# Second scores spread and attention transposed through DRAM scratch instead of TensorE, in a four-layer graph kernel

## The chip, the cores and the metric

The kernel runs on one core of a Trainium2 chip. The metric is the device time in microseconds (us), as the median of repeated executions. Everything is float32: the input holds 128 graphs of 128 nodes with 512 features each (32 MB), and the output has the same size.

## The reference, cut to what matters

Four graph layers run one after the other, each with a residual and a layer normalisation. The change touches layer 2, an attention layer, and what runs beside it.

```python
# layer 0: x = LN(x + adj @ x @ W0 + bias)
# layer 1: x = LN(x + rel @ v), rel = norm(adj.T * (q @ k.T)), q, k, v = x @ Wq.T, x @ Wk.T, x @ Wv.T
# layer 2 (a: 1024 numbers, mask = adj):
h = einsum('bnc,cf->bnf', x, W)
s1 = einsum('bnf,f->bn', h, a1)
s2 = einsum('bnf,f->bn', h, a2)
e = leaky_relu(s1[:, :, None] + s2[:, None, :], negative_slope=0.2)
e = e * mask[None, :, :]
att = softmax(e, axis=2)
h_prime = einsum('bij,bjf->bif', att, h)
x = LN(x + elu(h_prime + beta * h))
# layer 3: x = LN(x + max over features of relu(...))
```

In layer 2 the scores `s2[j]` have to stand along the free axis on all 128 partitions, because `e[i, j] = s1[i] + s2[j]` has node `i` on the partitions. The product `att @ h` needs the attention transposed, with `j` on the partitions. Both are moves of data across partitions.

## The kernel before: the parts concerned

The graphs are worked on in 32 groups of 4 (`G = 4`, `NG = 32`). Each group passes through all layers, and the groups are staggered: in one period of 28 table slots the kernel runs layer 0 of one group, layer 1 of the group before it, and layers 2 and 3 of earlier ones. `TABLE` gives for each step the slot, relative to the group's own start, at which its instructions are emitted; step `f` of group `g` is emitted at `28 * g + slot`. All pieces are then sorted by slot, and each engine keeps its instructions in that order. So slot 61.6 of group g, slot 33.6 of group g+1 and slot 5.6 of group g+2 are neighbours in every engine's queue.

```python
    TABLE = dict(
        load=[-20], y=row(0.5, 1), bias=row(1.3, 1), y_sums=row(5.2, 0.5), y_w=row(7, 1, 7),
        ...
        move=row(20.5, 0.1), x_sums=row(25.3, 0.5), m=row(28, 1, 7), scores=row(36.5, 1),
        masked=[39.95], squares=[40.4], turn_rel=[40.3],
        move_rel=row(41.2, 0.1), inverse=[42.5], v=row(42, 1, 7), attend=row(50.6, 1),
        residual=row(51.0, 1), dots=[51.7, 53.8, 54.9, 55.6], norm1=[54.6], scale=[57.2],
        apply1=row(65.4, 0.33),
        spread=[61.6], leaky=[62.0], weighted=[63.4], greatest=[64.3], exps=[64.4],
        divide=[65.8], turn_att=[68.6], with_beta=[69.0], gather=row(71.5, 1),
        z_sums=row(75.3, 0.5), z_w=row(77, 1, 7), exp=[87.5, 88.5, 90.4, 92.0],
        elu=[87.8, 89.4, 92.8, 93.8], norm2=[95.0], apply2=row(95.7, 0.33),
        ...
    )
```

The four large products (`y`, `m`, `v`, `z`) are done by a Strassen-like scheme of seven block products each. A block product is a step of 8 matmuls; its result goes to one of three regions, and the regions live in few PSUM buffers. In the steps' order 1, 2, 6, 5, 7, 3, 4, region 1 (step 2) and region 2 (steps 5 and 3) share a single buffer, `r12`, across all four products.

```python
    ORDER = (1, 2, 6, 5, 7, 3, 4)
    REGION = {1: 0, 6: 0, 7: 0, 4: 0, 2: 1, 5: 2, 3: 2}
    ...
        def step(i):
            ...
            if first:                                   # i in (1, 2, 5)
                r[where] = psum.tile([P, 2, H], FP,
                    tag="r0" if where == 0 else "r12", ...,
                    bufs=2 if where == 0 else 1)
            mul(r[where], s["f"][i], bw[w][i], first)   # 8 matmuls

        def out(i):
            p, dst = r[REGION[i]], c(*BLOCK[i])
            if fresh and i in (1, 6, 5, 4):
                act.copy(dst, p)
            else:
                dve.tensor_tensor(dst, p, dst, ALU.add)

        for n, i in enumerate(ORDER):
            emit(at[n], step, i)
            emit(at[n] + 0.72, out, i)
```

GpSimd forms the sums of blocks that the scheme needs (`y_sums`, `x_sums`, `z_sums`, four 128x512 operations per product). Layer 2 before the change:

```python
        def spread():                                   # TensorE: s2 onto all partitions
            s["p"] = bank(f"p_s2_{g}")
            for b in range(G):
                pe.transpose(s["p"][:, b * P : (b + 1) * P],
                    s12[g][:, 1, b : b + 1].to_broadcast([P, P]), ident)

        def leaky():
            e = work.tile([P, G, P], FP, tag="e", ...)
            dve.tensor_tensor(e, s["p"]..., s12[g][:, 0, :, None].to_broadcast([P, G, P]), ALU.add)
            dve.scalar_tensor_tensor(e, e, ALPHA, e, op0=ALU.mult, op1=ALU.max)

        def weighted():
            pool.tensor_tensor(s["e"], s["e"], adj_b, ALU.mult)

        def greatest():
            dve.tensor_reduce(s["nm"], s["e"], AX.X, ALU.max, negate=True)

        def exps(i):                                    # ScalarE: exp and its sum, one graph each
            ...
        def divide(i):
            dve.reciprocal(rs, s["sums"]...)
            engine = pool if n == G else dve            # GpSimd, but for the last group
            engine.tensor_tensor(e, e, rs[:, :, None].to_broadcast([P, n, P]), ALU.mult)

        def turn_att(i):                                # TensorE: attention transposed
            for b in ...:
                pe.transpose(s["p"][:, b * P : (b + 1) * P], s["e"][:, b, :], ident)

        def with_beta(i):
            dve.tensor_tensor(s["eT"]..., s["p"]..., beta_b..., ALU.add)

        def gather(b):                                  # TensorE: att @ x
            ...
        def elu(b):                                     # layer 2's end, VectorE
            dve.scalar_tensor_tensor(x, s["c", b], 0.0, x2[g][:, b, :], op0=ALU.max, op1=ALU.add)
            dve.scalar_tensor_tensor(x, s["m", b], 1.0, x, op0=ALU.min, op1=ALU.add)
            stats(s, f"2_{g}", b, x)                    # batch-norm statistics of the row
```

Of the kernel before, what the change touches and what calls it, by code (L numbers as in the profile page):

```python
# [8 lines left out]
FP = mybir.dt.float32  # L9
AF = mybir.ActivationFunctionType  # L10
ALU = mybir.AluOpType
# [18 lines left out]
def kernel(  # L30
# [33 lines left out]
    pe, dve, act, pool = (InOrder(tc, e) for e in (nc.tensor, nc.vector, nc.scalar, nc.gpsimd))  # L64
    sync = InOrder(tc, nc.sync)
    B, N, D = x.shape
    P = 128
    assert N == P and D % P == 0
    K = D // P
    Q = P // 32  # L70
    H = D // 2
    G = 4
    NG = B // G
# [4 lines left out]
    work = ctx.enter_context(tc.tile_pool(name="work", bufs=1))  # L78
    small = ctx.enter_context(tc.tile_pool(name="small", bufs=4))
    psum = ctx.enter_context(tc.tile_pool(name="psum", bufs=1, space=bass.MemoryType.PSUM))  # L80

    def bank(name):
        return psum.tile([P, D], FP, tag="ps", name=name, bufs=3)
# [40 lines left out]
    ident = const.tile([P, P], FP)  # L124
# [15 lines left out]
    beta_i = const.tile([P, P], FP)  # L140
# [79 lines left out]
    def emit(at, f, *args):  # L220
        pieces.append((at, lambda: f(*args)))

    def each(at, f):
        for b in range(len(at)):
            emit(at[b], f, b)

    def row(at, step, n=G):
        return [at + i * step for i in range(n)]


    TABLE = dict(
        load=[-20], y=row(0.5, 1), bias=row(1.3, 1), y_sums=row(5.2, 0.5), y_w=row(7, 1, 7),
        stats0=row(14.4, 0.4), norm0=[16.2], apply0=row(16.8, 0.33),
        turn=row(21.4, 1), turn_blocks=row(18.4, 0.6),
        move=row(20.5, 0.1), x_sums=row(25.3, 0.5), m=row(28, 1, 7), scores=row(36.5, 1),
# [1 line left out]
        move_rel=row(41.2, 0.1), inverse=[42.5], v=row(42, 1, 7), attend=row(50.6, 1),  # L237
        residual=row(51.0, 1), dots=[51.7, 53.8, 54.9, 55.6], norm1=[54.6], scale=[57.2],
        apply1=row(65.4, 0.33),
        spread=[61.6], leaky=[62.0], weighted=[63.4], greatest=[64.3], exps=[64.4],  # L240
        divide=[65.8], turn_att=[68.6], with_beta=[69.0], gather=row(71.5, 1),
        z_sums=row(75.3, 0.5), z_w=row(77, 1, 7), exp=[87.5, 88.5, 90.4, 92.0],
        elu=[87.8, 89.4, 92.8, 93.8], norm2=[95.0], apply2=row(95.7, 0.33),
        widen=[98.7, 100.0, 103.6, 104.6], top=[99.1, 100.4, 104.0, 105.0],
# [13 lines left out]
            greatest=[10.5], exps=[11.2], divide=[13.6], turn_att=[18.3], with_beta=[18.9],  # L258
            gather=row(36.7, 0.9), z_sums=row(39.95, 1.3),
# [6 lines left out]
            m=[0.0, 1.73, 3.46, 5.2, 7.4, 9.1, 10.8], scores=row(12.7, 0.9), masked=[16.4],  # L266
# [3 lines left out]
            greatest=[52.4], exps=row(53.2, 0.6), divide=row(53.9, 0.6),  # L270
            turn_att=row(54.4, 0.6), with_beta=row(54.9, 0.6), gather=[55.2, 56.1, 60.5, 65.0],
# [98 lines left out]
    def rows_of(t):  # L370
        return lambda nh, ch: t()[:, 2 * nh : 2 * nh + 2, H * ch : H * ch + H]


    def stats(s, g, b, t):
        if b == 0:
            s["mv"] = small.tile([P, G, 2], FP, tag="mv", name=f"mv_{g}", bufs=6)
        st = small.tile([P, 6], FP, tag="st", name=f"st_{g}_{b}")
        dve.bn_stats(st, t)
        dve.bn_aggr(s["mv"][:, b, :], st)
# [235 lines left out]
    s12 = {}  # L615
# [3 lines left out]

    def layer2(g, t):  # L620
        s = {}

        def spread():
            s["p"] = bank(f"p_s2_{g}")
            for b in range(G):
                pe.transpose(
                    s["p"][:, b * P : (b + 1) * P],
                    s12[g][:, 1, b : b + 1].to_broadcast([P, P]),
                    ident,
                )  # L630

        def leaky():
            e = work.tile([P, G, P], FP, tag="e", name=f"e_{g}")
            dve.tensor_tensor(
                e,
                s["p"].rearrange("p (b n) -> p b n", b=G),
                s12[g][:, 0, :, None].to_broadcast([P, G, P]),
                ALU.add,
            )
            dve.scalar_tensor_tensor(e, e, ALPHA, e, op0=ALU.mult, op1=ALU.max)  # L640
            s["e"] = e
# [5 lines that stand above are left out]
            s["nm"] = small.tile([P, G], FP, tag="nm", name=f"nm_{g}")  # L647
            dve.tensor_reduce(s["nm"], s["e"], AX.X, ALU.max, negate=True)

        def exps(i):  # L650
            if i == 0:
                s["sums"] = small.tile([P, G], FP, tag="sums", name=f"sums_{g}")
            for b in range(i * n, i * n + n):
                act.activation(
                    s["e"][:, b, :],
                    s["e"][:, b, :],
                    AF.Exp,
                    bias=s["nm"][:, b : b + 1],
                    accum_out=s["sums"][:, b : b + 1],
                )  # L660

        def divide(i):
            rs = small.tile([P, n], FP, tag=f"rs{n}", name=f"rs_{g}_{i}")
            dve.reciprocal(rs, s["sums"][:, i * n : i * n + n])
            e = s["e"][:, i * n : i * n + n, :]
            engine = pool if n == G else dve
            engine.tensor_tensor(e, e, rs[:, :, None].to_broadcast([P, n, P]), ALU.mult)

        def turn_att(i):
            if i == 0:  # L670
                s["p"] = bank(f"p_eT_{g}")
            for b in range(i * n, i * n + n):
                pe.transpose(s["p"][:, b * P : (b + 1) * P], s["e"][:, b, :], ident)

        def with_beta(i):
            if i == 0:
                s["eT"] = work.tile([P, G, P], FP, tag="eT", name=f"eT_{g}")
            dve.tensor_tensor(
                s["eT"][:, i * n : i * n + n, :],
                s["p"].rearrange("p (b n) -> p b n", b=G)[:, i * n : i * n + n, :],  # L680
                beta_b[:, i * n : i * n + n, :],
                ALU.add,
            )

        def gather(b):
            if b == 0:
                s["zT"] = work.tile([P, K, G * P], FP, tag="aT_yz", name=f"zT_{g}")
            p = bank(f"p_z_{g}_{b}")
            for k in range(K):
                pe.matmul(  # L690
                    p[:, k * P : (k + 1) * P],
                    x2[g][:, b, k * P : (k + 1) * P],
                    s["eT"][:, b, :],
                    start=True,
                    stop=True,
                )
            act.copy(
                s["zT"][:, :, b * P : (b + 1) * P], p.rearrange("p (k n) -> p k n", k=K)
            )

        def begin():
            s["c"] = work.tile([P, G, D], FP, tag="c", name=f"c_{g}")
            for b in range(G):
                s["c", b] = s["c"][:, b, :]

        def direct(b):

            s["c", b] = psum.tile([P, D], FP, tag="r0", name=f"c_{g}_{b}", bufs=2)
            for k in range(K):
                pe.matmul(  # L710
                    s["c", b],
                    s["zT"][:, k, b * P : (b + 1) * P],
                    w2_sb[:, k, :],
                    start=(k == 0),
                    stop=(k == K - 1),
                )

        def exp(b):
            s["m", b] = work.tile([P, D], FP, tag="m", name=f"m_{g}_{b}", bufs=3)
            act.activation(s["m", b], s["c", b], AF.Exp)  # L720

        def elu(b):
            if b == 0:
                x3[g] = data.tile([P, G, D], FP, tag="x3", name=f"x3_{g}")
            x = x3[g][:, b, :]
            dve.scalar_tensor_tensor(
                x, s["c", b], 0.0, x2[g][:, b, :], op0=ALU.max, op1=ALU.add
            )
            dve.scalar_tensor_tensor(x, s["m", b], 1.0, x, op0=ALU.min, op1=ALU.add)
            stats(s, f"2_{g}", b, x)  # L730

        n = G // len(t["exps"])
        emit(t["spread"][0], spread)
        emit(t["leaky"][0], leaky)
        emit(t["weighted"][0], weighted)
        emit(t["greatest"][0], greatest)
        each(t["exps"], exps)
        each(t["divide"], divide)
        each(t["turn_att"], turn_att)
        each(t["with_beta"], with_beta)  # L740
        each(t["gather"], gather)
        if g < NG - 1:
            left_factors(t["z_sums"], s, "zT", "s_yz", f"z_{g}", 0)
            product(t["z_w"], f"z_{g}", by_rows, s, "2", rows_of(lambda: s["c"]), True, begin)
        else:
            each(t["z_w"], direct)
        each(t["exp"], exp)
        each(t["elu"], elu)
        norm(t["norm2"], t["apply2"], s, f"2_{g}", lambda: x3[g])
# [107 lines left out]
```

## Time and profile before

| | before |
|---|---|
| median of 3 | 2218.47 us (2218.12 to 2219.33) |
| profiled span | 2214.6 us |
| mean granted TensorE clock | 0.996 |
| TensorE busy | 2170.9 us, 98% |
| VectorE busy | 1547.9 us, 70% |
| ScalarE busy | 1102.5 us, 50% |
| GpSimd busy | 907.7 us, 41% |
| transposes of `s2` (`p_s`) | 128 instructions |
| transposes of the attention (`p_eT`) | 128 instructions |

Engines are named PE (TensorE matmul), PEld (its weight load), DVE (VectorE), ACT (ScalarE), POOL (GpSimd) and SP (the engine that issues DMAs). In a row of the timeline the columns are the start in us, the time from the first instruction's start to the last one's end in us, the engine, a helper's line number (always the same here, so rows are told apart by tile names), the operation, output and inputs by the program's tile names, the shape, and the number of instructions merged in the row. A bracket at the end gives the idle time of the engine before the row and whom it waited for. Matmuls overlap their neighbours, so the time that a row takes on TensorE is the distance from its start to the next row's start, not its listed duration.

The tile names in the timeline: `r_m`, `r_y`, `r_v`, `r_z` are the PSUM regions of the four large products; `tT` is the result of `m`, `x` that of `y`; `s_y` and `yT` are what GpSimd's sums for `y` write; `p_s` and `p_eT` are the two groups of transposes; `e` is the attention.

### The profile page before, as it was taken

What the parts mean: (1) busy time and instruction counts of PE and PEld (TensorE: products, weight loads), DVE (VectorE), ACT (ScalarE), POOL (GpSimd) and SP (SyncE); (2) the same over time, 40 slices, a digit from 0 to 9 for tenths busy, and PEclk for the clock granted to TensorE, in tenths of its full rate; (3) what the DMA queues carried; (4) which work ended last, traced back from release to release, by engine and by line L of the source; (5) the groups of instructions that cost most, each with busy time, mean ns of one, the idle gap of its engine ahead of it and who ended that gap; (6) DMA issues with size and microseconds to landing.
All of it is one profiled execution on the core that took longest, in us unless ns stands there. A gap on an engine that the chain in (4) does not pass through costs nothing.

```text
span 2214.6 us, 31863 instructions
## 1 busy us (share of the span) xinstructions
PE 2170.9 (98%) x11073; PEld 1839.6 (83%) x11073; DVE 1547.9 (70%) x3290; ACT 1102.5 (50%) x2446; POOL 907.7 (41%) x743
## 2 busy tenths in 40 slices
PE   7999999999999999999999999999999999999996
PEld 5788888888888888888888888888888888888873
DVE  4657766767766767776767776767767677667676
ACT  2224445554445554445554445554455554455547
POOL 3334444334444344443344443344443344443321
PEclk9999999999999999999999999999999999999998
DMA  4011222211222211222112222112222112221101
GB/s 167 25 20 29 61 60 62 62 20 49 60 60 63 58 21 52 59 61 62 44 31 56 58 62 63 41 30 59 58 62 63 29 39 62 59 63 44 21 28 57
DMA packets 333295, 115.15 MB, mean 52 GB/s; under 512 B 297424, under 2 KB 297552, under 8 KB 333136
## 3 DMA queue, kind: packets, MB, share of 16 engines
q1 hardware_dynamic: 331936, 110.77, 19.7%
q10 hardware_dynamic: 1200, 2.36, 0.3%
q8 instruction: 88, 1.44, 0.3%
q14 instruction: 71, 0.58, 0.1%
HBM read 39.65 MB, written 33.55 MB: 33 GB/s over the span
## 4 chain that ended last, share of the span: by engine, by line
PE 93%; DVE 3%; ACT 2%; POOL 1%; issue 1%; DMA 0%; ACTq 0%; DVEq 0%; POOLq 0%
PE r_y L26 17%; PE r_v L26 17%; PE r_m L26 17%; PE r_z L26 17%; PE p_z L26 5%; PE p_rel L26 5%; PE p_y L26 5%; PE p_o L26 5%; PE p_a L26 5%; DVE x L26 1%; ACT x L26 1%; DVE st L26 1%; PE p_eT L26 1%; PE p_m L26 1%; PE p_s L26 1%
## 5 line engine op out<-in xcount | busy, mean ns | idle before, releaser
L26 ACT ACTIVATE x<-x,nmean,rstd 128x512 f32<-128x512 f32 x384 | 288.6, 808 | 120.8 <-DVE nmean L26 120.8
L26 DVE BATCH_NORM_STATS2 st<-x 128x6 f32<-128x512 f32 x384 | 263.8, 687 | 8.8
L26 POOL TENSOR_TENSOR x<-x,bias_sb 128x512 f32<-128x512 f32 x128 | 170.1, 1331 | 137.9 <-PE p_y L26 137.5
L26 DVE SCALAR_TENSOR_TENSOR x<-m,x 128x512 f32<-128x512 f32 x128 | 114.4, 894 | 108.5 <-ACT m L26 98.5
L26 POOL TENSOR_TENSOR s_x<-xT 128x512 f32<-128x512 f32 x64 | 82.2, 1285 | 261.1 <-DMA xT<-xB 250.2
L26 ACT COPY c<-r_z 128x512 f32<-128x512 f32 x124 | 71.2, 574 | 223.3 <-PE r_z L26 198.0
L26 ACT COPY yT<-p_y 128x512 f32<-128x512 f32 x128 | 75.1, 586 | 213.6 <-PE p_y L26 213.6
L26 POOL TENSOR_TENSOR rstd<-ve,mhalf 128x4 f32<-128x4 f32 (+1 forms) x99 | 98.5, 995 | 194.1 <-DVE ve L26 188.9
L26 DVE TENSOR_TENSOR x<-r_y,x 128x512 f32<-128x512 f32 x224 | 151.7, 678 | 31.2 <-PE r_y L26 31.0
L26 DVE SCALAR_TENSOR_TENSOR scr<-x,wa 128x512 f32<-128x512 f32 x256 | 161.5, 675 | 0.0
L26 DVE STREAM_TRANSPOSE xB<-x 128x512 f32<-128x512 f32 x120 | 81.2, 696 | 108.7 <-ACT x L26 97.7
L26 PEld LDWEIGHTS p_y<-adjT,x 128*128 128x128 f32 x1024 | 136.9, 196 | 11.2 <-ACT adjT L26 4.8
L26 POOL TENSOR_TENSOR s_z<-zT 128x512 f32<-128x512 f32 x31 | 39.4, 1270 | 255.9 <-ACT zT L26 255.9
L26 PE MATMUL p_y<-adjT,x 128*128 128x128 f32 x1024 | 137.6, 280 | 4.5 <-ACT adjT L26 4.5
L26 PEld LDWEIGHTS p_z<-eT,x 128*128 128x128 f32 x1024 | 134.0, 192 | 7.9 <-issue 1.0
L26 PEld LDWEIGHTS p_rel<-xT,tT 128*128 128x128 f32 x1024 | 134.1, 191 | 7.4 <-DVE tT L26 0.8
L26 DVE TENSOR_REDUCE mx<-p_a 128x1 f32<-128x512 f32 x128 | 88.3, 691 | 69.6 <-PE p_a L26 69.6
L26 PE MATMUL p_a<-x,adjT 128*128 128x512 f32 x256 | 130.8, 596 | 5.8 <-DVE mx L26 4.4
L26 ACT COPY tT<-r_m 128x512 f32<-128x512 f32 x128 | 75.6, 590 | 121.6 <-PE r_m L26 121.6
L26 PE MATMUL p_rel<-xT,tT 128*128 128x128 f32 x1024 | 134.9, 275 | 0.6 <-DVE tT L26 0.6
L26 PE MATMUL p_z<-eT,x 128*128 128x128 f32 x1024 | 134.7, 275 | 0.1
L26 PE MATMUL p_o<-v,relT 128*128 128x512 f32 x256 | 130.4, 593 | 0.3 <-ACT v L26 0.3
(129 smaller groups left out, 5268.6 us busy)
## 6 DMA issues: line engine op xcount, KB each, us to landing
out_dram<-x SPq DMA_DIRECT2D x128, 256.0 KB, 2.5
x<-in_x_dram SPq DMA_DIRECT2D x31, 1024.0 KB, 5.3
xT<-xB SPq DMA_DIRECT2D x480, 64.0 KB, 2.3
relT<-relB SPq DMA_DIRECT2D x512, 16.0 KB, 1.8
w_sb<-in_L_gnn_weight_dram ACTq DMA_DIRECT2D x1, 1024.0 KB, 5.6
x<-in_x_dram SPq DMA_DIRECT2D x4, 256.0 KB, 7.8
wq_sb<-in_L_gnn_Wq_dram SPq DMA_DIRECT2D x1, 1024.0 KB, 12.3
wk_sb<-in_L_gnn_Wk_dram SPq DMA_DIRECT2D x1, 1024.0 KB, 15.1
```

What stands on the lines that cost most here:

```text
L26: return lambda *args, **kw: self.tc.keep_in_program_order(op(*args, **kw))
```

## The change

For the groups 0 to 29 (the last two keep the old way, `late`), the eight transposes of each group leave TensorE. The scores `s2` are written to a 2 KB line in DRAM and read back with the same line on all partitions. The attention is divided and given its `beta * identity` in one VectorE pass (four instructions, which takes the division off GpSimd), transposed in 32x32 blocks by VectorE, written to DRAM and read back with the blocks exchanged, so that the whole 128x128 matrices come out transposed. To make room for the transfers, `spread` moves from slot 61.6 to 57.3, the softmax's steps go about one slot forward, and GpSimd's third and fourth sums for `y` go behind the mask product `weighted`. What it is for: TensorE is the busiest engine, and it is relieved of 240 of its 256 transposes in layer 2.

```diff
+    dram = ctx.enter_context(tc.tile_pool(name="dram", bufs=2, space=bass.MemoryType.DRAM))
...
-        load=[-20], y=row(0.5, 1), bias=row(1.3, 1), y_sums=row(5.2, 0.5), y_w=row(7, 1, 7),
+        load=[-20], y=row(0.5, 1), bias=row(1.3, 1), y_sums=[5.2, 5.7, 6.9, 7.4], y_w=row(7, 1, 7),
...
-        spread=[61.6], leaky=[62.0], weighted=[63.4], greatest=[64.3], exps=[64.4],
-        divide=[65.8], turn_att=[68.6], with_beta=[69.0], gather=row(71.5, 1),
+        spread=[57.3], leaky=[61.2], weighted=[62.1], greatest=[63.1], exps=[63.2],
+        divide=[64.8], turn_att=[68.6], with_beta=[69.0], turn_blocks_2=[65.4], move_2=[65.5], gather=row(71.5, 1),
...
     def layer2(g, t):
+        late = g >= NG - 2
         def spread():
-            s["p"] = bank(f"p_s2_{g}")
-            for b in range(G): pe.transpose(...)
+            if late:
+                ...                                     # as before
+            else:
+                line = dram.tile([P, G], FP, tag="s2", name=f"s2d_{g}")
+                sync.dma_start(line, s12[g][:, 1, :])
+                wide = work.tile([P, P, G], FP, tag="s2", name=f"s2_{g}")
+                sync.dma_start(
+                    wide.rearrange("p n b -> p (n b)"),
+                    line.rearrange("n b -> (n b)")[None, :].to_broadcast([P, P * G]),
+                )
+                s["s2"] = wide.rearrange("p n b -> p b n")
...
         def divide(i):
             dve.reciprocal(rs, s["sums"][:, i * n : i * n + n])
+            if not late:
+                for b in range(G):
+                    e = s["e"][:, b, :]
+                    dve.scalar_tensor_tensor(
+                        e, e, rs[:, b : b + 1], beta_i, op0=ALU.mult, op1=ALU.add
+                    )
+                return
...
+        def turn_blocks():
+            s["eB"] = work.tile([P, Q, G, P // Q], FP, tag="eB", name=f"eB_{g}")
+            dve.transpose(
+                s["eB"].rearrange("p q b u -> p b q u"),
+                s["e"].rearrange("p b (q u) -> p b q u", q=Q),
+            )
+
+        def move():
+            m = P // Q
+            blocks = dram.tile([P, Q, G * m], FP, tag="eB", name=f"eBd_{g}")
+            sync.dma_start(blocks, s["eB"].rearrange("p q b u -> p q (b u)"))
+            eT = work.tile([P, Q, G, m], FP, tag="eT", name=f"eT_{g}")
+            for q in range(Q):
+                sync.dma_start(
+                    eT[q * m : (q + 1) * m].rearrange("p a b u -> p a (b u)"),
+                    blocks.rearrange("(a j) q n -> q j a n", a=Q)[q],
+                )
+            s["eT"] = eT.rearrange("p a b u -> p b a u")
...
-        each(t["turn_att"], turn_att)
-        each(t["with_beta"], with_beta)
+        if late:
+            each(t["turn_att"], turn_att)
+            each(t["with_beta"], with_beta)
+        else:
+            emit(t["turn_blocks_2"][0], turn_blocks)
+            emit(t["move_2"][0], move)
```

## The prediction

> **What bounds it.** I read the page's busy shares and chain first, then the timeline of TensorE over one period, then VectorE and GpSimd over the stretch in which the change moves things.
>
> ```profile
> PE 2170.9 (98%) x11073; PEld 1839.6 (83%) x11073; DVE 1547.9 (70%) x3290; ACT 1102.5 (50%) x2446; POOL 907.7 (41%) x743
> ...
> PE 93%; DVE 3%; ACT 2%; POOL 1%; issue 1%; DMA 0%; ACTq 0%; DVEq 0%; POOLq 0%
> ```
>
> TensorE is busy 98% of the span and makes 93% of the chain. A busy share can hide stalls, so I add up a period. The first `p_s` transpose of a group starts at 987.8 us and that of the next at 1054.4, about 66.8 us later. In the timeline a block product takes 1.73 us from start to next start, a pair of `p_a` or `p_o` 0.86, eight matmuls of `p_y`, `p_rel` or `p_z` 0.89. A period holds 28 block products (48.4), four pairs each of `p_a` and `p_o` (6.9), four eights of each of the three others (10.7) and the transposes (0.9): 66.9 us. The whole period is TensorE's own work; there is no stall in it.
>
> TensorE's timeline in one period:
>
> ```profile
> 1052.68 1.89 PE L26 MATMUL r_m<-s_x,m_qk 128*128 128x256 f32 x8
> 1054.40 0.60 PE L26 MATMUL p_s<-ident,d 128*128 128x128 f32 x4
> 1054.84 1.89 PE L26 MATMUL r_m<-xT,t_m 128*128 128x256 f32 x8
> 1056.57 3.62 PE L26 MATMUL r_y<-w_sb,yT 128*128 128x256 f32 x16
> ...
> 1070.50 0.60 PE L26 MATMUL p_eT<-ident,e 128*128 128x128 f32 x4
> 1070.94 1.89 PE L26 MATMUL r_y<-t,yT 128*128 128x256 f32 x8
> ```
>
> Four `p_s` take 1054.84 - 1054.40 = 0.44 us, four `p_eT` likewise. What matters below: the rows of 1052.68 are step 3 of `m` (region 2), those of 1054.84 step 4, and the sixteen at 1056.57 are steps 1 and 2 of `y`. Step 2 of `y` starts at 1056.57 + 1.73 = 1058.30, and its region shares the one `r12` buffer with region 2 of `m`. So it may start only when VectorE has read step 3 of `m` out. VectorE's timeline:
>
> ```profile
> 1052.95 0.69 DVE L26 TENSOR_TENSOR tT<-r_m,tT 128x512 f32<-128x512 f32 x1 [1.15 <-PE r_m L26]
> 1053.56 0.70 DVE L26 SCALAR_TENSOR_TENSOR x<-c,x 128x512 f32<-128x512 f32 x1
> 1054.36 1.57 DVE L26 SCALAR_TENSOR_TENSOR x<-m,x 128x512 f32<-128x512 f32 x1
> 1055.96 0.69 DVE L26 BATCH_NORM_STATS2 st<-x 128x6 f32<-128x512 f32 x1
> 1056.69 0.18 DVE L26 BATCH_NORM_AGGREGATE mv<-st 128x2 f32<-128x6 f32 x1
> 1056.79 0.66 DVE L26 TENSOR_TENSOR tT<-r_m,tT 128x512 f32<-128x512 f32 x1
> 1057.37 0.68 DVE L26 TENSOR_TENSOR e<-p_s,d 128x512 f32<-128x512 f32 x1
> 1058.08 0.76 DVE L26 SCALAR_TENSOR_TENSOR e<-e 128x512 f32<-128x512 f32 x1
> 1058.76 0.68 DVE L26 TENSOR_TENSOR x<-r_y,x 128x512 f32<-128x512 f32 x1
> ```
>
> The read-out of step 3 is the `tT` of 1056.79, done at 1057.45: 0.85 us before step 2 of `y` wants the buffer. The `tT` of 1052.95 (step 7) had to wait for TensorE, so VectorE cannot be early here. From there to 1075 it has hardly a gap. GpSimd beside it:
>
> ```profile
> 1052.43 1.28 POOL L26 TENSOR_TENSOR s_y<-yT 128x512 f32<-128x512 f32 x1
> 1053.79 1.59 POOL L26 TENSOR_TENSOR s_y<-s_y,yT 128x512 f32<-128x512 f32 x1
> 1055.34 1.72 POOL L26 TENSOR_TENSOR yT<-yT 128x512 f32<-128x512 f32 x1
> 1057.02 1.27 POOL L26 TENSOR_TENSOR s_y<-yT,s_y 128x512 f32<-128x512 f32 x1
> 1058.92 1.27 POOL L26 TENSOR_TENSOR e<-e,adj_sb 128x512 f32<-128x512 f32 x1 [0.63 <-DVE e L26]
> ```
>
> **What the skill says.** The Trainium skill, "SBUF — State Buffer", section "Who interferes with whom": a VectorE instruction with two SBUF inputs and a GpSimd instruction that reads SBUF exclude each other, and the loser waits for the whole instruction. The trace agrees: `x<-m` takes 1.57 instead of 0.69 us and goes on when the second sum ends, about 1055.34; the sums take 1.59 and 1.72 instead of 1.27. "TensorE: Matmul & The Clock Gate", section "Part 4: PE-mode transpose", gives about 275 ns for a transpose in one kernel. The row here has 273 ns, but 0.44 / 4 = 0.11 us is what one takes of the pipeline, and I count that. "DMA: Bandwidth & Descriptors", section "Two DMAs through the same engine are not ordered", says that a dependent DMA has to wait for the first one's completion semaphore; so each detour costs two landings in a row. No run here shows such a pair yet. Single landings were 1.8 us (16 KB, `relT`), 2.3 (64 KB, `xT`) and 2.5 (256 KB, `out`).
>
> **The change part by part.** Removed on TensorE: 30 groups x 8 transposes x 0.11 = 26.4 us. With nothing else, 2192.1 us, 1.2% less; this is the most that it can bring.
>
> The `s2` detour: `d` is ready at 1045.03 (the last small VectorE step on `d` starts at 1044.86). Write of 2 KB, say 2 us, then read of 256 KB, 2.5 us, and some 0.6 us of issue each: there by 1051. VectorE wants it at 1053.56. Hidden, with 2 to 3 us in hand.
>
> `leaky` goes from slot 62.0 to 61.2, and the read-out of step 3 of `m` stands at 61 + 0.72 = 61.72, the `elu` pass of the second graph at 61.4. So in VectorE's order the two `leaky` instructions come in front of `x<-c`, `x<-m`, the statistics and that read-out. From start to next start they took 0.71 + 0.68 = 1.39 us. The read-out ends at 1057.45 + 1.39 = 1058.84, while TensorE, with `p_s` gone, comes to step 2 of `y` at 1058.30 - 0.44 = 1057.86. That is a stall of 1.0 us where there was none.
>
> Then the shared port. `leaky`'s first instruction now has both inputs in SBUF and runs at 1053.56 to 1054.25; the second sum gets in behind it and ends about 1055.35. The second `leaky` instruction has two SBUF inputs and waits for that, until about 1055.95 (it takes the collision that `x<-m` had). Now `weighted` is free to start on GpSimd, just as `x<-c` runs: it starts about 1056.6 and ends about 1057.75, and `x<-m` waits for it, some 0.9 us again. So two collisions in place of one: the read-out ends near 1059.8, and the stall is about 1.9 us.
>
> Behind it VectorE gets more work in the same stretch: four divisions for 128x128 (I take 0.2 us each, an estimate from the four 128x128 transposes `relB` in 0.90 us) and a 128x512 block transpose (0.70 as `xB`), with the wait for the reciprocal some 1.7 us, in front of the read-outs of steps 6, 5 and 7 of `y`. Counted from the start A of step 2 of `y`, with TensorE's rows: step 3 of `y` at A + 10.5, its buffer read out at A + 10.2; step 4 at A + 12.2, the read-out it waits for (step 7, behind a 1.0 us `rstd` on GpSimd) at A + 12.2. Zero to 0.2 us more; I take 0.1. `with_beta` (0.67) goes, but only after that.
>
> The attention's detour: blocks transposed at about A + 6.7, write landed at A + 9.2, four reads issued 0.6 to 0.7 us apart as the `relT` ones are (16 in 11.3 us), landed at A + 14. `gather` comes at A + 18.3. Hidden. The `relT` transfers start up to 2 us later; their data is needed 23 us after.
>
> Sum per group: -0.88 + 1.9 + 0.1 = +1.1 us; over 30 groups +33 us: 2251 us. Since TensorE has no slack anywhere in the period, a stall of this kind is not made good later.
>
> **Rivals.** (1) The stall does not come, and the transposes' 26 us are simply gained: 2192 us. For it: TensorE's share, and the care with which the slots were moved. Against it: the order of instructions and the single `r12` buffer are fixed by the program, and 1.39 + 0.44 is more than the 0.85 us in hand. (2) The stall comes without a second collision, because `weighted` slips in elsewhere: 1.0 + 0.1 - 0.88 = +0.2, 2225 us. Only the order of arrival at the port speaks for it. (3) A DMA becomes the bound: if the broadcast read, in which 128 partitions read the same 2 KB, takes 3 us longer than thought, `leaky` and all behind it slip and each us costs 30 us: 2280 us or more. Against it: transfers are idle in this stretch (DMA share 0.00 from 1052.68 to 1058.29), and the margins are 2 to 4 us. (4) VectorE becomes the bound over the whole stretch of `y`, with several small stalls: 2265 us.
>
> **Range and chances.** 2251 us. The range of 8 in 10 goes from 2206, between the rivals 1 and 2, to 2272, a stall of 2.7 us. Faster by 2% would be 2174, below what the removal can give: 0.02. Slower by 2% is 2263, a stall of 2.4 us: 0.25. The rest, 0.73, is within 2%.
>
> **What would show it.** Right: `p_s` and `p_eT` keep 8 instructions each; TensorE has about 30 waits `r_y` on VectorE's `tT`, some 50 to 60 us in total; a period of about 68 us; `e<-e` or `x<-m` at 1.5 us beside GpSimd's `s_y` and `e`. Wrong: no such wait and a period of 66.0 us, or waits of `p_z` on `eT` or of VectorE's `e` on the DMA of `s2`.

## The result, and the profile after

| | before | after |
|---|---|---|
| median | 2218.9 us (2218.12 to 2219.41) | 2276.58 us (2275.22 to 2277.93) |
| ratio | 1 | 1.026 (95% interval 1.0242 to 1.0278) |
| profiled span | 2214.6 us | 2273.5 us |
| TensorE busy | 2170.9 us, 98% | 2170.3 us, 95% |
| granted TensorE clock, mean | 0.996 | 0.991 |
| steady period of a group | 66.81 us | 68.64 us; 69.94 us for five groups |

The kernel became 57.7 us slower (2276.58 - 2218.9). That lies 4.6 us above the top of the predicted range.

The page after, its busy shares and its chain by engine:

```profile
PE 2170.3 (95%) x10833; PEld 1821.9 (80%) x10833; DVE 1595.8 (70%) x3410; ACT 1099.5 (48%) x2446; POOL 895.3 (39%) x713
...
PE 88%; DVE 7%; ACT 2%; issue 1%; POOL 1%; DMA 1%; ACTq 0%; DVEq 0%; POOLq 0%
```

TensorE has 240 matmuls less (11073 - 10833), yet its listed busy time is the same: its other rows have become longer by about as much. VectorE has come from 3% to 7% of the chain. The page's group of the first two steps of `y` says where:

```profile
L26 PE MATMUL r_y<-w_sb,yT 128*128 128x256 f32 x512 | 126.5, 391 | 62.3 <-DVE tT L26 62.3
```

TensorE idles 62.3 us in front of this group, released by VectorE's `tT`, in 30 waits. In a typical period TensorE's timeline reads:

```profile
1357.53 1.89 PE L26 MATMUL r_y<-w_sb,yT 128*128 128x256 f32 x8
1361.49 1.99 PE L26 MATMUL r_y<-w_sb,yT 128*128 128x256 f32 x8 [2.08 <-DVE tT L26]
1363.32 1.05 PE L26 MATMUL p_rel<-xT,tT 128*128 128x128 f32 x8
...
1371.18 1.05 PE L26 MATMUL p_rel<-xT,tT 128*128 128x128 f32 x8
1372.17 1.97 PE L26 MATMUL r_y<-w_sb,s_y 128*128 128x256 f32 x8
1374.05 1.99 PE L26 MATMUL r_y<-t,yT 128*128 128x256 f32 x8
1375.88 1.89 PE L26 MATMUL r_v<-wvT,xT 128*128 128x256 f32 x8
```

Before, steps 1 and 2 of `y` were one unbroken row of sixteen. Now step 2 starts at 1361.49 instead of 1357.53 + 1.73 = 1359.26: 2.23 us late (the bracket's 2.08 counts from the modelled end of the row before). Smaller losses follow. Step 2 itself, the first block product after the wait, takes 1.83 instead of 1.73 us: 0.10. The last `p_rel` takes 0.99 instead of 0.89, and steps 3 and 4 take 1.88 and 1.83: 0.35 together. VectorE's timeline beside it:

```profile
1354.34 0.69 DVE L26 TENSOR_TENSOR tT<-r_m,tT 128x512 f32<-128x512 f32 x1 [1.15 <-PE r_m L26]
1354.95 1.06 DVE L26 TENSOR_TENSOR e<-s,d 128x512 f32<-128x512 f32 x1
1356.05 1.60 DVE L26 SCALAR_TENSOR_TENSOR e<-e 128x512 f32<-128x512 f32 x1
...
1358.35 1.57 DVE L26 SCALAR_TENSOR_TENSOR x<-m,x 128x512 f32<-128x512 f32 x1
...
1360.78 0.66 DVE L26 TENSOR_TENSOR tT<-r_m,tT 128x512 f32<-128x512 f32 x1
```

The two `leaky` rows (`e<-s,d` and `e<-e`) now stand in front of the read-out of step 3 of `m` (1360.78), the addition with which VectorE takes the finished product out of PSUM and so frees the `r12` buffer. Two rows are long, 1.60 and 1.57 us. On GpSimd the second sum and the mask product run at those moments:

```profile
1355.18 1.91 POOL L26 TENSOR_TENSOR s_y<-s_y,yT 128x512 f32<-128x512 f32 x1
1357.72 1.65 POOL L26 TENSOR_TENSOR e<-e,adj_sb 128x512 f32<-128x512 f32 x1 [0.63 <-DVE e L26]
```

`e<-e` is held up by the first of these until about 1357.0, `x<-m` by the second until about 1359.3; undisturbed both take 0.69 us.

### The profile page after: what moved, and what is told of

Read it like the earlier page. It is cut to its first block, busy times and chain, and to the rows that moved or that the text cites. A ratio compares the mean times of both kernels' runs of the same rounds, so it can differ in the third digit from the quotient of the medians.

```text
span 2273.5 us, 31832 instructions
## 1 busy us (share of the span) xinstructions
PE 2170.3 (95%) x10833; PEld 1821.9 (80%) x10833; DVE 1595.8 (70%) x3410; ACT 1099.5 (48%) x2446; POOL 895.3 (39%) x713
## 4 chain that ended last, share of the span: by engine, by line
PE 88%; DVE 7%; ACT 2%; issue 1%; POOL 1%; DMA 1%; ACTq 0%; DVEq 0%; POOLq 0%
PE r_v L26 16%; PE r_z L26 16%; PE r_m L26 16%; PE r_y L26 15%; PE p_rel L26 5%; PE p_z L26 5%; PE p_y L26 5%; PE p_o L26 5%; PE p_a L26 4%; DVE x L26 3%; DVE st L26 2%; DVE tT L26 1%; ACT x L26 1%; ACT tT L26 1%; PE p_m L26 1%
## 5 line engine op out<-in xcount | busy, mean ns | idle before, releaser
L26 DVE TENSOR_TENSOR x<-r_y,x 128x512 f32<-128x512 f32 x224 | 150.9, 675 | 57.5 <-PE r_y L26 57.3
L26 PE MATMUL r_y<-w_sb,yT 128*128 128x256 f32 x512 | 126.5, 391 | 62.3 <-DVE tT L26 62.3
L26 PEld LDWEIGHTS r_y<-w_sb,yT 128*128 128x128 f32 x512 | 95.6, 192 | 86.2 <-DVE tT L26 74.3
```

Of the source, the lines that this page charges most:

```text
L26: return lambda *args, **kw: self.tc.keep_in_program_order(op(*args, **kw))
```

## The experiments

The theory from the prediction: TensorE waits for the single `r12` buffer, since `leaky` stands in front of its read-out, and collisions with GpSimd at the port to SBUF that both share stretch that. The rivals: the landing of the DRAM transfers sets the pace, or VectorE's added work does, wherever it stands. All runs were compared with the kernel before on the same chip.

| run | what differs | median, us | ratio to before (95%) |
|---|---|---|---|
| changed kernel | | 2276.58 | 1.0242 to 1.0278 |
| `order_back` | `leaky`, `greatest`, `exps` behind the read-outs | 2277.81 | 1.0251 to 1.0285 |
| `slots_alone` | new slots, no DRAM | 2253.6 | 1.0143 to 1.0173 |
| `unit_stride` | scores laid out graph by graph | 2470.64 | 1.112 to 1.1154 |
| `divide_late` | divisions and block transpose later | 2260.69 | 1.0175 to 1.0206 |
| `sum_behind` | one GpSimd sum later | 2243.34 | 1.0099 to 1.013 |
| `old_slots` | old slots, divisions later | 2232.32 | 1.0047 to 1.008 |
| `best_try` | the same, two graphs' `exp` and `elu` earlier | 2199.32 | 0.9899 to 0.9928 |
| `best2` | the same, block transpose later still | 2196.71 | 0.9886 to 0.9916 |
| `before_early` | kernel before, `exp` and `elu` earlier | 2217.3 | 0.9988 to 1.0005 |
| `scores_only` | only the scores through DRAM | 2208.17 | 0.9936 to 0.9965 |
| `attention_only` | only the attention through DRAM | 2203.3 | 0.9916 to 0.9949 |

### order_back: the three steps put back behind the read-outs

```diff
-        leaky=[61.2], weighted=[62.1], greatest=[63.1], exps=[63.2],
+        leaky=[61.8], weighted=[62.1], greatest=[63.8], exps=[63.9],
```

> Changed kernel with only the places of three steps put back behind the read-outs: leaky 61.2 to 61.8 (behind the read-out of step 3 of m), greatest 63.1 to 63.8 and exps 63.2 to 63.9 (behind that of step 1 of y). Theory 1 (TensorE waits for the r12 buffer because leaky stands in front of the read-out): the 30 waits of r_y step 2 on tT, 2.2 us each, are gone; what is left are waits of about 1.5 us per group at steps 7, 3 and 4 of y, because VectorE now has the four divisions and the block transpose in front of their read-outs; time near 2238 us. Theory 2 (the DRAM detour's landing times or VectorE's added work as a whole set the period): leaky later makes all behind it later, 2276 us or more.

Measured 2277.81 us: no gain. It looks like theory 2, but TensorE's timeline shows more:

```profile
1358.66 3.62 PE L26 MATMUL r_y<-w_sb,yT 128*128 128x256 f32 x16
...
1367.36 1.05 PE L26 MATMUL p_rel<-xT,tT 128*128 128x128 f32 x8
1370.49 1.97 PE L26 MATMUL r_y<-t,yT 128*128 128x256 f32 x8 [2.08 <-DVE x L26]
```

The wait at step 2 of `y` is gone, as theory 1 says: the sixteen are one row again. In its place step 7 waits for the read-out of step 6, 2.24 us (1370.49 - 1367.36 - 0.89). On VectorE this read-out stands behind a `x<-c` of 1.78 us and behind the divisions and the block transpose:

```profile
1364.27 1.78 DVE L26 SCALAR_TENSOR_TENSOR x<-c,x 128x512 f32<-128x512 f32 x1
...
1367.89 1.14 DVE L26 SCALAR_TENSOR_TENSOR e<-e,rs,beta_i 128x128 f32<-128x128 f32 x4
...
1369.06 0.71 DVE L26 STREAM_TRANSPOSE eB<-e 128x512 f32<-128x512 f32 x1
1369.70 0.65 DVE L26 TENSOR_TENSOR x<-r_y,x 128x512 f32<-128x512 f32 x1
```

The `x<-c` is long because GpSimd's last sum runs beside it:

```profile
1364.21 1.28 POOL L26 TENSOR_TENSOR s_y<-yT,s_y 128x512 f32<-128x512 f32 x1
```

This collision is new: with `leaky` later, the mask product and the two sums behind it come later too. It makes 1.10 of the 2.24 us (1.78 - 0.68); without it the read-out would still be 1.1 us late, behind the divisions and the block transpose. So the order in front of step 3's read-out is one cause, and VectorE's added work is a second one. In the changed kernel the second costs 0.35 us; that the first stall hides the rest there, since VectorE catches up while TensorE stands still, is read from the two timelines and was not tested. The expectation had put 1.5 us at these steps, without the collision.

### slots_alone: the new slots without any DRAM

```diff
-        late = g >= NG - 2
+        late = True
-        spread=[57.3], leaky=[61.2], ...
+        spread=[60.9], leaky=[61.2], ...
```

> Only the new slots, no DRAM: all groups keep both sets of transposes on TensorE (spread at 60.9, so that the scores are there for leaky at 61.2). Theory 1 (order alone makes the stall): the wait at step 2 of y comes all the same, about 1.6 us per group (leaky's first instruction reads PSUM and takes 0.7 instead of 1.07 us), nothing is removed from TensorE, and the divisions stay on GpSimd so that there are no waits at steps 3 and 4: 2218 + 30 x 1.6 = 2266 us. Theory 2 (DRAM detour is the cause): no wait, 2218 us.

Measured 2253.6 us, 34 us more than before with not one DMA added. The wait is at the same place:

```profile
1344.38 1.89 PE L26 MATMUL r_y<-w_sb,yT 128*128 128x256 f32 x8
1347.26 1.99 PE L26 MATMUL r_y<-w_sb,yT 128*128 128x256 f32 x8 [0.99 <-DVE tT L26]
```

1347.26 - 1344.38 - 1.73 = 1.15 us, and 29 x (1.15 + 0.10) = 36 us, against 34 measured: the whole loss. The DRAM detour is not needed for the stall. The stall is below the expected 1.6 us, and 1.08 below the changed kernel's 2.23. The timelines have three differences. TensorE still does `p_s` (0.44 us) and so comes to step 2 later. `leaky`'s first instruction, which reads PSUM here, takes 0.68 instead of 1.06 us. And `e<-e` takes 1.32 instead of 1.60 us, since GpSimd's second sum now runs beside that first instruction without waiting and is over sooner (1.27 us long instead of 1.91). Together they make 1.10 us.

### unit_stride: consecutive scores for leaky

```diff
-                line = dram.tile([P, G], ...)
-                sync.dma_start(line, s12[g][:, 1, :])
-                wide = work.tile([P, P, G], ...)
+                line = dram.tile([G, P], ...)
+                sync.dma_start(line.rearrange("b n -> n b"), s12[g][:, 1, :])
+                wide = work.tile([P, G, P], ...)
```

> Changed kernel, with the scores laid out in DRAM and in SBUF graph by graph, so that leaky's first instruction reads consecutive numbers and not every fourth one. Theory A (the step of 16 bytes between elements makes that instruction 1.07 instead of 0.69 us): it falls to 0.69 us, the stall at step 2 of y from 2.23 to about 1.85 us, time 2276 - 11 = 2265 us. Theory B (it is long because it shares the port with GpSimd's sum): still 1.07 us and 2276 us. The clock's drop after the stall may become rarer or vanish with the shorter stall: a further 0 to 6 us.

The instruction fell to 0.69 us, as theory A says. That it takes 1.07 us with GpSimd idle too is seen in `order_back`, where GpSimd waits for `leaky` and the instruction still has 1.066 us in the median. So the step of 16 bytes is the cause. But the time went to 2470.64 us, for a reason that was not expected: the write of the line is now made of 512 single numbers instead of 128 runs of four. The DMA issue of the write, with the size in KB and the median time to landing in us:

```profile
s2d<-d SPq DMA_DIRECT2D x30, 2.0 KB, 8.6
```

and the waits of this run, who for whom, with the sum in us, the number and the longest:

```profile
PE r_y L26 <- DVE tT L26: 208.9, 30, 8.2
...
DVE e L26 <- DMA s<-s2d: 182.0, 30, 7.4
```

The same 2 KB took 8.6 us to land instead of 1.4. `leaky` waited 182 us in all, and TensorE 209 us behind it. This is what rival 3 of the prediction would have looked like; in the changed kernel `leaky` waits for the scores once, for 0.2 us. Because the late scores cover everything else, this run does not tell what the slow read costs the kernel.

### divide_late: only the divisions and the block transpose moved

```diff
-        divide=[64.8], ..., turn_blocks_2=[65.4], move_2=[65.5], ...
+        divide=[67.05], ..., turn_blocks_2=[67.1], move_2=[67.2], ...
```

> Changed kernel with only the divisions and the block transpose moved behind the read-out of step 5 of y (divide 64.8 to 67.05, block transpose 65.4 to 67.1, transfer 65.5 to 67.2); leaky stays where the change put it. If the stall at step 2 of y comes from leaky alone, it stays at 2.2 us per group and only the small waits at steps 3 and 4 of y go (0.35 us per group in the changed kernel): 2266 us. If VectorE's added work is what sets the period, it falls below 2225 us.

2260.69 us, 16 us less than the changed kernel. The stall at step 2 is untouched, as TensorE's waits show:

```profile
PE r_y L26 <- DVE tT L26: 62.1, 30, 2.1
```

The small waits of steps 3 and 4 are gone: the period is 68.29 us (step 2 starts at 1352.86 and 1421.15), 0.35 us below 68.64, which is 10 us over the run. Most of the other 6 us is the clock's: it drops once in these periods instead of five times, at 1.3 us each, see below.

### sum_behind: one GpSimd step out of leaky's way

```diff
-        y_sums=[5.2, 5.7, 6.9, 7.4]
+        y_sums=[5.2, 6.3, 6.9, 7.4]
```

> Changed kernel with one GpSimd step moved: the second sum for y goes behind the mask product (5.7 to 6.3), so that GpSimd is idle while leaky's second instruction runs. If the port is the cause of the two long VectorE instructions, that instruction falls from 1.59 to 0.69 us, the read-out of step 3 of m comes 0.9 us sooner, the stall at step 2 of y falls from 2.2 to 1.3 us and the time to about 2247 us; the clock's drops, which follow the long stall, would be rarer. If the port has nothing to do with it, 2276 us.

2243.34 us, 33 us less. VectorE's timeline:

```profile
1337.35 1.07 DVE L26 TENSOR_TENSOR e<-s,d 128x512 f32<-128x512 f32 x1
1338.45 0.69 DVE L26 SCALAR_TENSOR_TENSOR e<-e 128x512 f32<-128x512 f32 x1
...
1339.85 1.57 DVE L26 SCALAR_TENSOR_TENSOR x<-m,x 128x512 f32<-128x512 f32 x1
```

`e<-e` is at 0.69 us; `x<-m`, still beside the mask product, is at 1.57. Step 2 of `y` is 1.35 us late (1343.00 - 1339.92 - 1.73), 0.88 less than in the changed kernel; 29 x 0.88 = 26 us, and the clock drops, some 6 us, are gone as well. The collision with the second sum is shown by this; that with the mask product is read from the timeline alone.

### old_slots, best_try and best2: all causes taken away

`old_slots` puts `leaky` to `exps` and GpSimd's sums back to the slots of before and keeps the divisions late. `best_try` also moves two steps into a gap of VectorE:

```diff
-        exp=[87.5, 88.5, 90.4, 92.0], elu=[87.8, 89.4, 92.8, 93.8]
+        exp=[85.9, 86.1, 90.4, 92.0], elu=[86.5, 87.2, 92.8, 93.8]
```

and `best2` has the block transpose at 67.8 and its transfer at 67.85.

> Both DRAM detours kept, with the slots of before for leaky, weighted, greatest, exps and GpSimd's sums, and the divisions and the block transpose at 67.05 and 67.1; exp and elu stay where they were. If the two causes together (leaky in front of the read-out of step 3 of m, divisions in front of that of step 6 of y) are all there is, 2195 to 2202 us; if VectorE still lacks room without the earlier exp and elu, about 2225 us, with waits at steps 7, 3 or 4 of y.

> Both DRAM detours kept, old slots for leaky (62.0), weighted, greatest, exps and GpSimd's sums; divide and block transpose moved behind the read-out of step 5 of y and behind the small step that GpSimd's rstd waits for (67.05, 67.1, transfer 67.2); exp and elu of the first two graphs moved forward (exp 87.5, 88.5 to 85.9, 86.1; elu 87.8, 89.4 to 86.5, 87.2) into a stretch in which VectorE waits 3.8 us for ScalarE. Theory 1: no wait of TensorE on VectorE is left, period 66.0 us, time 2192 to 2196 us, 1.1% less than before. Theory 2 (detour or added work cannot be hidden): above 2218 us, with waits of p_z on eT or of e on the transfer of s2.

> The best try with one more step moved: the block transpose and its transfer behind the read-out of step 7 of y (67.1 to 67.8, 67.2 to 67.85). In the best try TensorE still waits 0.13 us per group at step 4 of y for that read-out, which stands behind the block transpose (0.64 us). If that is the rest, it goes: 2195 us. The attention then lands 0.6 us later, with 1.4 us in hand; if the margin is smaller than the trace says, p_z waits on eT and the time is above 2199 us.

`old_slots` came to 2232.32 us, so the expectation missed: order and division slots are not all. TensorE still waits:

```profile
1347.65 1.99 PE L26 MATMUL r_y<-t,yT 128*128 128x256 f32 x8 [0.66 <-DVE x L26]
```

Step 4 of `y` waits for the read-out of step 7 in each group, because VectorE's added work has no room left in the stretch from step 7 of `m` to step 4 of `y`. That work is the divisions, the block transpose and `leaky`'s first instruction, which takes 1.80 us here (0.68 before). Now that it reads two SBUF inputs, it not only has the slow read: it starts at 1333.79, while GpSimd's last sum runs from 1333.45 to 1334.72. `best_try` makes room: 2199.32 us, some 3 us above the expected range, and no matmul waits in each group any more; only the weight loads of step 4 still wait for the read-out of step 7, 8.9 us in 29 times. `best2`, in which these are gone too, reaches 2196.71 us, 0.990 of before, with a period of 1386.10 - 1320.16 = 65.94 us, which is 66.81 less the two removed sets of 0.44, to 0.01 us:

```profile
1320.16 1.89 PE L26 MATMUL r_y<-w_sb,s_y 128*128 128x256 f32 x8
...
1386.10 1.89 PE L26 MATMUL r_y<-w_sb,s_y 128*128 128x256 f32 x8
```

It stays 4.6 us above the 2192.1 that the removal alone would give. The difference is not in the steady period. The traces put most of it at the start: step 2 of `y` of the fourth group starts at 193.16 us, before at 189.09. At the same step of the group ahead of it TensorE waits 1.89 us (1.46 before), and behind that wait the clock drops, which it does not before.

### before_early, scores_only, attention_only: what the gain is made of

> Control: the kernel before with nothing but exp and elu of the first two graphs moved forward as in the best try. TensorE had no waits in its period, so nothing is to be had: 2218 us, the same. If it gets faster by more than 5 us, the gain of the best try is not that of the removed transposes.

> Only the scores go by way of DRAM, in the slots of the best try; the attention is divided on GpSimd and transposed on TensorE as before. If the removed transposes alone count (four per group, 0.44 us, 30 groups = 13 us) and the detour is hidden: 2206 us. If leaky's slower read (1.07 instead of 0.68 us) or the landing costs something on the path: above 2212 us.

> Only the attention goes by way of DRAM, in the slots of best2; the scores are spread by TensorE as before. If the removed transposes alone count: 2206 us as well, and the two halves add up to the whole. If VectorE's divisions and block transpose cost time even here: above 2212 us.

The earlier `exp` and `elu` alone give nothing (2217.3 us, interval around 1), as was expected of a period full of TensorE's own work. The scores' detour alone gives 10.5 us (2218.62 - 2208.17), the attention's alone 15.3 (2218.62 - 2203.3); together 25.8, against 21.9 for both in `best2`. The steady period is 66.37 us in both halves, 0.44 below the 66.81 of before. So the removed transposes are the gain, about 13 us a set. That the scores' half stays some 3 us short, as `best2` does, is again the start: its fourth group's step 2 of `y` starts at 192.90 us, that of `attention_only` at 189.19. Chance has a part in these times, for `before_early`, which is no faster than the kernel before, has 190.45. The 2 us by which the attention's half exceeds 13 stay open.

## Why the prediction was wrong, step by step

The path was right: TensorE waits for the one `r12` buffer, because `leaky` and two collisions stand in front of its read-out. What failed are sizes in its sum per group: the stall was put at 1.9 us and measured 2.23, the added work at 0.1 and measured 0.35, the slower step behind the wait (0.10 us) was left out, and so were the clock's drops (6.5 us in all).

**What bounds the kernel: right.** The period was full, and every us that TensorE waits in it is lost once per group. `before_early` agrees: more room on VectorE alone brings nothing. (The 987.8 us from which the prediction took its period is a slip. The first `p_s` starts at 987.59, which gives 66.81.)

**The removed transposes, 26.4 us: right.** `best2`'s period is shorter by 0.87 us, the prediction had 0.88.

**The stall at step 2 of `y`: right in its place and its cause, too small.** Foreseen 1.9 us, measured 2.23. The term that was mis-sized is `leaky`'s first instruction: the prediction gave it the 0.69 us of the PSUM version, and the read with a step of 16 bytes takes 1.07. Laid over the timeline of before at step 7's read-out (1354.34 on 1052.95), GpSimd's second sum ends 0.35 us later than foreseen, `e<-e` 0.31 and the read-out 0.25. That the slow read moves the rest is read from this timeline; no run has shown it alone. The two collisions came as foreseen (1.60 and 1.57 us). Not foreseen was that step 2 itself then takes 0.10 us longer.

**The added work behind it: 0.1 us foreseen, 0.35 measured.** `divide_late` moves this work behind the read-out of step 5, and its period is 0.35 us shorter. Rival 4 came true to this extent. The divisions were put at 0.2 us each from the block transposes `relB`; from start to next they take 0.26 (1366.65 to 1367.71 for four), and from the reciprocal's start to the row behind the block transpose 1.99 us go by (1366.47 to 1368.46), not 1.7. With the margins near zero that the prediction had worked out itself, this showed fully. In `order_back` the same work costs more, about 1.1 us at one step.

**Rival 3, the transfers: did not happen, but was nearer than foreseen.** The broadcast read took 5.2 us to land instead of the assumed 2.5, the write 1.4 instead of 2. In the typical period the read was issued at 1347.87 and landed 5.5 us later, about 1353.4; `leaky` started at 1354.95. In hand were 1.5 us, less than the 2 to 3. The attention's detour was hidden, as foreseen.

**Not foreseen: the clock.** In five of the groups the period is 69.94 instead of 68.64 us. Here is a stretch behind the wait in one of them, as the windows' view has it: from the left the stretch and its length, TensorE's busy time and number of matmuls, the granted clock, the DMA share and GB/s.

```profile
1088.06:1089.76 1.70, 1.70 (x9) 0.50 0.00 0
```

After the wait TensorE runs at half its clock for a while: eight `p_rel` take 1.70 instead of 0.89 us. It costs 1.3 us a time, 6.5 us in all.

**The sum.** The first group waited at step 2 of `y` in both kernels (1.46 us listed before, 1.58 after), so 29 groups count: 29 x (2.23 + 0.10 + 0.35) = 77.7, less 26.4, plus 6.5 for the clock: 57.8 us, against 57.7 measured. (So close an agreement is luck; the two profiled spans differ by 58.9.) Foreseen were 33. Of the missing 25 us about 10 (29 x 0.33) are the longer stall, put down to the strided read; 3 (29 x 0.10) the slower step 2; 7 (29 x 0.25) the divisions and the block transpose; 6.5 the clock. Counting 29 groups instead of 30 takes some 2 off.

## What to carry to other kernels

Before a step is moved forward in the queue of a busy engine, look for what it passes: a read-out that frees a buffer with a single copy is worth more than its 0.6 us, because the next product waits for it. When the bounding engine has no slack in its period, work taken off it is a gain only if the engines that took it over had a gap at that very place; the average share (70% for VectorE) says nothing of it, and the timeline from one read-out to the next does. And where one stall is removed without gain, see whether a second stood behind it: here three causes had to go together.

## What the runs showed of the hardware

**The clock after a short wait depends on when the wait falls.** The changed kernel waits 2.2 us in 29 groups. Behind five of these waits, those that end at 259.4, 672.5, 1085.7, 1498.8 and 1775.0 us, the clock falls to half, each time for 3.41 us. `divide_late` has the same 29 waits but one drop, behind the first (190.3 us). `order_back`, with 2.2 us at step 7, has six. `slots_alone` and `sum_behind`, with 1.15 and 1.35 us, have none in their steady periods; `unit_stride`, with about 7 us, drops in every group. The Trainium skill, "TensorE: Matmul & The Clock Gate", section "What's actually happening", says that a free-running window of 3413 ns decides the clock. The trace agrees with that: the five drops begin at 260.85, 673.86, 1086.88, 1499.89 and 1776.37 us, that is 121.0, 121.0, 121.0 and 81.0 such windows apart. Cut into such windows, counted from a drop, the traces of the changed kernel, `order_back` and `divide_late` show more. In the window ahead of each of the twelve drops TensorE's listed idle time was at least 1.97 us; where a wait was shared by two windows and neither held more than 1.95 us of it, no drop came. This also explains `divide_late`: its 68.29 us are 20.0 windows, so after its one drop the wait stays near one place in the window, with at most 1.55 us in one. The same section puts the half clock after at least one idle window of about 3.4 us; here some 2 us of idle time in a window were enough. The ends of matmuls are modelled, so the 2 us are rough, and no run moved the wait within the window with all else equal.

**A step of 16 bytes between elements makes a VectorE addition of 128x512 slower,** 1.07 us in `order_back` instead of 0.69 in `unit_stride`, both with no GpSimd instruction beside it.

**Two forms of DMA were dearer than their size says.** A write of 2 KB as single numbers took 8.6 us to land, as runs of 16 bytes 1.4. One 2 KB line read onto 128 partitions took 5.2 us in the median (4.1 to 5.9), where 256 KB of `out` took 2.5. The form may not be the only reason: in all groups but the last a load of 1 MB is issued 0.4 us behind this read.

**VectorE and GpSimd exclude each other at their shared port.** The Trainium skill, "SBUF — State Buffer", section "Who interferes with whom", says that a VectorE instruction with two SBUF inputs contends with a GpSimd instruction that reads SBUF, and calls the shared ports an exclusive lock. `sum_behind` agrees: one GpSimd operation moved, one VectorE instruction 0.9 us shorter (0.69 instead of 1.60 us). The wait there lasted to the end of the other's instruction: `e<-e`, which needs 0.69 us, ended at 1357.65 and so went on about 1356.96; the sum ended at 1357.09.
